# Query projection in units of two batch entries with 256-column matmuls, and value products by half blocks

## The chip, the core and the metric

One NeuronCore of a Trainium2 chip runs the whole kernel. The metric is the device time of one launch in microseconds; three timed runs of the kernel before lie between 2101.3 and 2101.5 us. Everything is computed in float32.

## The reference

One block of a recurrent model on `x` with 8 batch entries of 256 tokens and 512 features: a layer norm, multi-head latent attention with 128 heads, and a feed-forward gate. Cut to what matters here (the FFN gives `g`, and the output is `x + s * g`):

```
c_q  = xn @ Wq_down;  c_kv = xn @ Wkv_down            # latent 64
q_c  = (c_q @ Wq_up).reshape(b, s, 128, 4)            # k_c, v_c from c_kv the same way
q_r  = (xn @ Wq_rope).reshape(b, s, 128, 64)          # 512 x 8192 weights: the largest product
k_r  = xn @ Wk_rope                                    # one 64-wide key for all heads
scores = (q_c . k_c + q_r . k_r) / sqrt(68)
out  = softmax(scores) @ v_c
s    = out.reshape(b, s, 512) @ Wo
```

## The kernel before

There are two stages. The first (`first_phase`) takes the tokens 512 at a time: it normalizes and transposes `x`, makes the latent activations (`down`) and the rope key (`narrow`), and computes the FFN gates into DRAM. Its four passes call `between`, which sets up and starts the second stage: weights, first activations, and in the last pass the first projections.

The second stage is a loop over 64 blocks, `blocks = [(b, sg)]`: one batch entry and 16 of the 128 heads, entry after entry. A block has two halves. One half puts on TensorE (PE), in this order:

- `score` twice (L621): scores of four head groups at a time. Four matmuls with 32 rows each run side by side in the array's four row groups, 256 key columns each. Part 0 is the latent part (`qcm`, `kc`), parts 1 and 2 are the even and odd rope components (`qr`, `act`).
- one `Project` (L162 in `product`): half of the next block's rope queries. The even and odd weight columns, the two halves of the 512 features and the two 128-token halves make a 2 x 2 by 2 x 2 block product, done with seven products instead of eight. Four products go in `first`, three in `second`, each into its own PSUM bank. Each product is four 128x128 weight tiles (`u`, `c`) against 128 token columns. Some of the weights are read with a step of two (`quarter_w`, `w[..., a::2]`); others are sums of weights (`sum_w`, made on GpSimd for the first entry and read back from `sums_d` afterwards). `take` (ScalarE), `join` (GpSimd), the copy in `second` (ScalarE) and `end` (VectorE) put the results together in `qr`.
- at the end of a first half, every second block, `prepare` (L250, L251): the latent queries and keys; `spread` (GpSimd) puts the masked copies in `qcm`.
- at the end of a second half, `weigh` of the block before (L661): value products, with four 32-column weight tiles side by side in the array's column groups, 256 query columns each, summed over eight key groups. Once per entry `values` (L277) makes the values and `place_values` (GpSimd, L292) puts a block's values in `vpad`.

Meanwhile VectorE reduces the maxima (L633), ScalarE makes the exponentials (L639), and VectorE transposes them 32x32 (L649) into `pt`. `normalize` (VectorE) divides, and `finish` (L705) multiplies by `Wo`, multiplies by the gate and adds `x`; it runs in blocks 2 and 3 of the next entry. Each engine follows the written order. All eight PSUM banks are handed out in turn (`bank`): a `score` pair takes eight, a `Project` four, so the banks of the first four scores must have been read by `exponentials` before `first` can begin. Every fp32 matmul of the program is two passes on the PE, each with its own weight load.

All DMAs go through SyncE (SP) in written order: `load_rope` fetches the 1 MB of weights for the half after next, `sum_w` their sums, `load_act` an entry's activations, `load_out` gate and `x` for `finish`.

Of the kernel before, what the change touches and what calls it, by code (L numbers as in the profile page):

```python
# [33 lines left out]
def mla_ffn_gate_kernel(  # L34
# [42 lines left out]
    acts_d = [dram.tile([P, 5, S], F32, name=f"act_d{b}") for b in range(B)]  # L77
    krs_d = [dram.tile([R, TB], F32, name=f"kr_d{n}") for n in range(NTB)]

    sums_d = [dram.tile([P, 4, 2, 2, P], F32, name=f"sums_d{n}") for n in range(16)]  # L80
    gates_d = [dram.tile([P, D], F32, name=f"gate_d{n}") for n in range(NT // P)]

    actp = pool("act", 2)
    wp = pool("wrope", 2)
    qcp = pool("qc", 2)
    qrp = pool("qr", 2)
    vp = pool("v", 2)
    wsp = pool("wsum", 2)
    xsp = pool("xsum", 2)
# [8 lines left out]
    blocks = [(b, sg) for b in range(B) for sg in range(8)]  # L98
    acts, qks, qcms, valls, vpad_of, ropes, qrs = {}, {}, {}, {}, {}, {}, {}

    def load_act(b):
        if b < B:
            acts[b] = actp.tile([P, 7, S], F32, tag="act", name=f"act_{b}")
            nc.sync.dma_start(out=acts[b][:, 0:5, :], in_=acts_d[b])

            kr = krs_d[b // 2].rearrange("(a i) s -> i a s", a=2)[:, :, ds(b % 2 * S, S)]
            for r in range(4):
                nc.sync.dma_start(out=acts[b][32 * r : 32 * r + 32, 5:7, :], in_=kr)

    def load_rope(n, hf):  # L110

        if n < len(blocks):
            t = wp.tile([P, KT, 2, 4 * R], F32, tag="w", name=f"w_{n}_{hf}")
            nc.sync.dma_start(
                out=t.rearrange("p c q m -> p c (q m)"), in_=w_rope[blocks[n][1], hf]
            )
            ropes[n, hf] = t
# [4 lines left out]
    def quarter_w(w, a, k, u):  # L122

        return w[:, 2 * k : 2 * k + 2, u, a::2]

    wsums, xsums = {}, {}

    def sum_w(n, hf):

        if n >= len(blocks):  # L130
            return
        b, sg = blocks[n]
        t = wsp.tile([P, 4, 2, 2, P], F32, tag="ws", name=f"ws_{n}_{hf}")
        if b == 0:
            w = ropes[n, hf]
            q = lambda a, k: w[:, 2 * k : 2 * k + 2, :, a::2]
            nc.gpsimd.tensor_add(t[:, 0], q(1, 0), q(1, 1))
            nc.gpsimd.tensor_sub(t[:, 1], t[:, 0], q(0, 0))
            nc.gpsimd.tensor_sub(t[:, 2], q(0, 0), q(1, 0))
            nc.gpsimd.tensor_sub(t[:, 3], q(0, 1), t[:, 1])  # L140
            nc.sync.dma_start(out=sums_d[2 * sg + hf], in_=t)
        else:
            nc.sync.dma_start(out=t, in_=sums_d[2 * sg + hf])
        wsums[n, hf] = t

    def sum_x(b):

        if b < B:
            t = xsp.tile([P, 4, 2, P], F32, tag="xs", name=f"xs_{b}")
            q = lambda k, tau: acts[b][:, 2 * k : 2 * k + 2, ds(tau * P, P)]  # L150
            nc.gpsimd.tensor_sub(t[:, 0], q(0, 1), q(0, 0))
            nc.gpsimd.tensor_sub(t[:, 1], q(1, 1), t[:, 0])
            nc.gpsimd.tensor_sub(t[:, 2], q(1, 1), q(0, 1))
            nc.gpsimd.tensor_sub(t[:, 3], q(1, 0), t[:, 1])
            xsums[b] = t

    def product(bank_, w, x, first):


        for u in range(2):  # L160
            for c in range(2):
                nc.tensor.matmul(  # L162
                    bank_[:, ds(u * P, P)],
                    w(u)[:, c],
                    x[:, c],
                    start=first and u == 0 and c == 0,
                    stop=c == 1,
                    skip_group_check=True,
                )

    class Project:


        def __init__(self, n, hf):
            self.n, self.hf = n, hf
            self.b = blocks[n][0]
            self.w = ropes[n, hf]
            self.s, self.t = wsums[n, hf], xsums[self.b]
            if hf == 0:

                qrs[n] = qrp.tile([P, 2, 8, 4, 32], F32, tag="qr", name=f"qr_{n}")

            self.banks = []
            self.e = [
                qtp.tile([P, 2 * P], F32, tag=f"e{i}", name=f"e{i}_{n}_{hf}") for i in range(4)
            ]

        def x(self, k, tau):
            return acts[self.b][:, 2 * k : 2 * k + 2, ds(tau * P, P)]

        def a(self, a, k):
            return lambda u: quarter_w(self.w, a, k, u)

        def sums(self, i):
            return lambda u: self.s[:, i, :, u, :]

        def out(self, a, tau):
            q = qrs[self.n][:, a, 4 * tau : 4 * tau + 4, 2 * self.hf : 2 * self.hf + 2, :]
            return q.rearrange("p q u i -> p u q i")

        def split(self, t):
            return t.rearrange("p (u q i) -> p u q i", u=2, i=32)

        def first(self):

            for i, (w, x) in enumerate((
                (self.a(0, 0), self.x(0, 0)),
                (self.sums(1), self.t[:, 1]),
                (self.sums(2), self.t[:, 2]),
                (self.sums(0), self.t[:, 0]),  # L210
# [352 lines left out]
    def between(step):  # L563
# [7 lines left out]
        elif step == 2:  # L571
# [5 lines left out]
            for hf in range(2):  # L577
                sum_w(0, hf)
# [264 lines left out]
```

## Time and profile before

| | |
|---|---|
| median of three runs | 2101.48 us |
| the profiled execution: time, span | 2100.38 us, 2098.6 us |
| first stage | 0 to 231.9 us |
| block loop up to block 63 | 231.9 to 2053.5 us |
| block 63 and what follows | 2053.5 to 2098.6 us |
| PE matmul busy, weight loads busy | 2072.3 us (99%), 1713.9 us (82%) |
| VectorE, ScalarE, GpSimd busy | 1530.7, 1092.8, 713.4 us |
| DMA | 310.99 MB, engines 42% busy in the block loop |
| granted PE clock | 0.998 |

Matmul durations overlap, because a matmul's row runs from its start to its modelled end. The pace of a stream is therefore read from the starts: duration of a merged row less that of one matmul, divided by the number less one. A row's "PE" and "PEld" parts are matmul and weight load.

### The profile page before, as it was taken

How to read it: one execution, taken by the hardware profiler on the slowest of the kernel's cores; microseconds unless marked ns; L12 is line 12 of the kernel's file. 1: busy time of each engine (PE TensorE's matmuls, PEld its weight loads, DVE VectorE, ACT ScalarE, POOL GpSimd, SP SyncE). 2: the span in 40 equal slices, each digit the busy share in tenths (PEclk: the TensorE clock that was granted, in tenths of full speed). 3: DMA queues.
4: the chain of work that ended last, by engine and by line, in shares of the span. 5: the costliest groups of instructions: out<-in, count | busy, mean ns of one | idle time of the engine just before them, and what ended most of it. 6: DMA issues, size and time to landing. Idle time of an engine off the chain costs nothing.

```text
span 2098.6 us, 60067 instructions
## 1 busy us (share of the span) xinstructions
PE 2072.3 (99%) x25024; PEld 1713.9 (82%) x25024; DVE 1530.7 (73%) x2601; ACT 1092.8 (52%) x2989; POOL 713.4 (34%) x989
## 2 busy tenths in 40 slices
PE   7999999999999999999999999999999999999997
PEld 3434888888889888898888988888888888888884
DVE  4332578778687777887777768778787777777875
ACT  2222455555456554564555545555455555554553
POOL 4226566632322233223332332233322333323221
PEclk9999999999999999999999999999999999999999
DMA  4132344343533444334444353444434444334330
GB/s 146 68 133 88 141 162 162 141 189 147 197 134 150 162 164 167 150 134 180 152 162 161 124 205 125 162 161 155 161 139 161 171 160 162 135 149 177 137 132 21
DMA packets 61362, 310.99 MB, mean 148 GB/s; under 512 B 7898, under 2 KB 15706, under 8 KB 28324
## 3 DMA queue, kind: packets, MB, share of 16 engines
q1 hardware_dynamic: 61092, 307.15, 39.3%
q8 instruction: 199, 3.26, 0.6%
q14 instruction: 71, 0.58, 0.1%
HBM read 276.19 MB, written 30.93 MB: 146 GB/s over the span
## 4 chain that ended last, share of the span: by engine, by line
PE 97%; DVE 1%; DMA 1%; POOL 0%; ACT 0%; issue 0%; SPq 0%; POOLq 0%; ACTq 0%; DVEq 0%
PE q L162 40%; PE sc L621 32%; PE av L661 11%; PE po L705 2%; PE px L443 2%; PE py L444 2%; PE pf L486 1%; PE px L429 1%; PE pm L397 1%; PE vps L277 1%; PE qk L250 1%; PE qk L251 1%; PE pp L397 1%; PE pm L458 1%; PE xpt L380 0%; DVE nmx L633 0%
## 5 line engine op out<-in xcount | busy, mean ns | idle before, releaser
L639 ACT ACTIVATE pr<-sc,nmx 128x256 f32<-128x256 f32 x2048 | 819.8, 504 | 415.3 <-DVE nmx L633 414.5
L633 DVE TENSOR_REDUCE nmx<-sc 128x2 f32<-128x512 f32 x1024 | 635.8, 684 | 356.5 <-PE sc L621 329.9
L649 DVE STREAM_TRANSPOSE pt<-pr 128x512 f32<-128x512 f32 x1024 | 635.3, 678 | 0.0
L621 PE MATMUL sc<-act,qr 32*128 32x256 f32 x8192 | 534.6, 374 | 0.0
L621 PEld LDWEIGHTS sc<-act,qr 32*128 32x128 f32 x8192 | 421.1, 185 | 22.1
L221 POOL TENSOR_TENSOR e<-e,e 128x256 f32<-128x256 f32 x128 | 93.2, 729 | 941.3 <-issue 499.9
L162 PE MATMUL q<-xs,ws 128*128 128x128 f32 x3072 | 364.0, 275 | 0.0
L162 PEld LDWEIGHTS q<-xs,ws 128*128 128x128 f32 x3072 | 353.1, 192 | 0.0
L621 PE MATMUL sc<-kc,qcm 32*128 32x256 f32 x4096 | 329.1, 387 | 0.1
L162 PEld LDWEIGHTS q<-act,w 128*128 128x128 f32 x2048 | 261.3, 196 | 44.3 <-ACT pr L639 42.7
L162 PE MATMUL q<-act,w 128*128 128x128 f32 x2048 | 296.2, 288 | 1.1 <-ACT pr L639 1.1
L621 PEld LDWEIGHTS sc<-kc,qcm 32*128 32x128 f32 x4096 | 199.5, 184 | 53.6 <-issue 29.7
L661 PE MATMUL av<-pt,vpad 128*32 128x256 f32 x4096 | 237.4, 382 | 3.8 <-DVE pt L649 2.7
L673 ACT ACTIVATE acc<-av,sides_sb 128x256 f32<-128x256 f32 x128 | 53.8, 471 | 315.2 <-DVE outT L688 161.4
L216 ACT COPY e<-q 128x256 f32<-128x256 f32 x512 | 205.5, 402 | 10.6 <-PE q L162 5.9
L661 PEld LDWEIGHTS av<-pt,vpad 128*32 128x32 f32 x4096 | 128.9, 110 | 89.8 <-issue 3.1
L162 PE MATMUL q<-xs,w 128*128 128x128 f32 x1024 | 141.5, 281 | 0.0
L162 PE MATMUL q<-act,ws 128*128 128x128 f32 x1024 | 135.2, 275 | 0.0
L162 PEld LDWEIGHTS q<-xs,w 128*128 128x128 f32 x1024 | 130.7, 196 | 0.0
L262 POOL TENSOR_TENSOR qcm<-qc,mask_sb 128x1024 f32<-128x1024 f32 x64 | 121.3, 1896 | 20.6 <-ACT qc L253 19.1
L162 PEld LDWEIGHTS q<-act,ws 128*128 128x128 f32 x1024 | 124.4, 192 | 0.0
L292 POOL COPY vpad<-vall 32x128 f32<-32x128 f32 x256 | 78.3, 306 | 95.7 <-PE av L661 51.6
(98 smaller groups left out, 1372.4 us busy)
## 6 DMA issues: line engine op xcount, KB each, us to landing
w<-in_w_rope_dram SPq DMA_DIRECT2D x128, 1024.0 KB
ws<-sums_d SPq DMA_DIRECT2D x112, 1024.0 KB
sums_d<-ws SPq DMA_DIRECT2D x16, 1024.0 KB
act_d<-act SPq DMA_DIRECT2D x8, 640.0 KB
act<-act_d SPq DMA_DIRECT2D x8, 640.0 KB
xt<-in_x_dram SPq DMA_DIRECT2D x16, 256.0 KB
gate_d<-gs SPq DMA_DIRECT2D x16, 256.0 KB
g<-gate_d SPq DMA_DIRECT2D x16, 256.0 KB
```

Of the source, the lines that this page charges most:

```text
L162: nc.tensor.matmul(bank_[:, ds(u * P, P)], w(u)[:, c], x[:, c], start=first and u == 0 and c == 0, stop=c == 1, skip_group_check=True,)
L216: nc.scalar.copy(self.e[i], self.banks[i])
L221: nc.gpsimd.tensor_add(m6, m6, m1)
L262: nc.gpsimd.tensor_mul(qcm, qks[b, sg // 2][0].rearrange("p (q i) -> p q i", i=32).unsqueeze(2).to_broadcast([P, 8, 4, 32]), mask_sb[:, ds ...
L292: nc.gpsimd.tensor_copy(vpad[rows, :, :, 8 * t + 4 * (n % 2) :][..., :4], valls[b][rows, :, sg])
L397: nc.tensor.matmul(ps, weights[:, c, :], xnT[tb][:, c, :], start=(c == 0), stop=(c == KT - 1))
L621: nc.tensor.matmul(sc[r][:, h, :], lhs.rearrange("p t i -> p (t i)"), rhs, start=(part == 0), stop=(part == 2),)
L633: nc.vector.tensor_reduce(nmx[:, r, :], scs[n, f][r], AX.X, ALU.max, negate=True)
L639: nc.scalar.activation(p[:, h, :], scs[n, f][r][:, h, :], AF.Exp, bias=nmxs[n, f][:, r, h : h + 1])
L649: nc.vector.transpose(pts[n, r].rearrange("p k q i -> p q k i")[:, ds(2 * f, 2)], prs.pop((n, f, r)).rearrange("p h (k j) -> p h k j", j=32),)
L661: nc.tensor.matmul(av[32 * r : 32 * r + 32, :S], vpad[:, k, r, :], pt[r][:, k].rearrange("p q i -> p (q i)"), start=(k == 0), stop=(k == 7),)
L673: nc.scalar.activation(a, av[:, :S], AF.Copy, scale=sides_sb[:, side : side + 1])
```

## The change

Blocks are taken in pairs: the two entries of a pair alternate within each `sg`, so `blocks` has entry 2p and 2p+1 of one head group after each other. A unit `j` of `Project` now serves both entries: it covers a quarter of a head group pair's weights and 2 x 256 tokens. The 2 x 2 split over the tokens is now the entry (`e`) and no longer the half of the tokens. A product is two weight tiles against 256 columns instead of four against 128. A block's half still has one unit, but the units run a pair of blocks ahead: `j = 2n + half + 4`, so four units lie in the first stage where two halves lay, and the last two blocks have none.

With it go: weights and sums in pieces of 512 KB (32 sums instead of 16); the activation sums made in the first stage by `sum_x` from `down`, stored as `xs_d`, and read back per pair with `load_xs` into the single buffer of `xsp`; `prepare` two blocks ahead; `values` for two entries in the first stage; the scores' loop with the part outermost; `pt` by half blocks in three buffers; `weigh` in two halves of 128 query columns, moved with `normalize` and `place_values` to the end of the first half; `finish` in second halves of the next pair's blocks 1 to 4, so that both finishes of entry 6 move behind the loop. The core of the diff:

```diff
@@ -74,19 +74,20 @@
     dram = pool("dram", 1, space=bass.MemoryType.DRAM)
-    acts_d = [dram.tile([P, 5, S], F32, name=f"act_d{b}") for b in range(B)]
+    xs_d = [dram.tile([P, 7, 2, S], F32, name=f"xs_d{n}") for n in range(NTB)]
+    cs_d = [dram.tile([P, TB], F32, name=f"cs_d{n}") for n in range(NTB)]
...
-    sums_d = [dram.tile([P, 4, 2, 2, P], F32, name=f"sums_d{n}") for n in range(16)]
+    sums_d = [dram.tile([P, 4, 2, P], F32, name=f"sums_d{n}") for n in range(32)]
-    actp = pool("act", 2)
+    actp = pool("act", 4)
-    qrp = pool("qr", 2)
+    qrp = pool("qr", 4)
-    xsp = pool("xsum", 2)
+    xsp = pool("xsum", 1)
...
+    blocks = [(2 * p + e, sg) for p in range(B // 2) for sg in range(8) for e in range(2)]
+    units = 4 * len(blocks) // 2
...
+    def load_rope(j):
+        if j < units:
+            t = wp.tile([P, KT, 4 * R], F32, tag="w", name=f"w_{j}")
+            sg, u = j // 4 % 8, j % 4
+            nc.sync.dma_start(out=t, in_=w_rope[sg, u // 2][:, :, ds(u % 2 * 4 * R, 4 * R)])
+            ropes[j] = t
+    def sum_w(j):
+        if j < units:
+            t = wsp.tile([P, 4, 2, P], F32, tag="ws", name=f"ws_{j}")
+            if j < 32:
+                q = lambda a, k: ropes[j][:, 2 * k : 2 * k + 2, a::2]
+                nc.gpsimd.tensor_add(t[:, 0], q(1, 0), q(1, 1))
...
+                nc.sync.dma_start(out=sums_d[j], in_=t)
+            else:
+                nc.sync.dma_start(out=t, in_=sums_d[j % 32])
+            wsums[j] = t
+    def sum_x(p, xnT):
+        q = lambda k, e: xnT[:, 2 * k : 2 * k + 2, ds(e * S, S)]
+        t = xsp.tile([P, 7, 2, S], F32, tag="xs", name=f"xt_{p}")
+        nc.gpsimd.tensor_sub(t[:, 3], q(0, 1), q(0, 0))
...
+        for i, of in enumerate((q(0, 0), q(1, 0), q(1, 1))):
+            nc.sync.dma_start(out=xs_d[p][:, i], in_=of)
+        nc.sync.dma_start(out=xs_d[p][:, 3:7], in_=t[:, 3:7])
+    def load_xs(p):
+        if p < B // 2:
+            xsums[p] = xsp.tile([P, 7, 2, S], F32, tag="xs", name=f"xs_{p}")
+            nc.sync.dma_start(out=xsums[p], in_=xs_d[p])
+    def product(bank_, w, x, first):
+        for c in range(2):
+            nc.tensor.matmul(
+                bank_,
+                w[:, c],
+                x[:, c],
+                start=first and c == 0,
+                stop=c == 1,
+                skip_group_check=True,
             )
...
     class Project:
...
+        def __init__(self, j):
+            self.j = j
+            self.n, self.u = 2 * (j // 4), j % 4
+            w, self.s = ropes[j], wsums[j]
+            self.a = lambda a, k: w[:, 2 * k : 2 * k + 2, a::2]
+            self.x = xsums[j // 32]
+            if self.u == 0:
+                for n in (self.n, self.n + 1):
+                    qrs[n] = qrp.tile([P, 2, 8, 4, 32], F32, tag="qr", name=f"qr_{n}")
+            self.e = [qtp.tile([P, S], F32, tag=f"e{i}", name=f"e{i}_{j}") for i in range(4)]
+        def out(self, a, e):
+            return qrs[self.n + e][:, a, :, self.u, :]
...
         def first(self):
...
+            for i, (w, x) in enumerate(
+                ((self.a(0, 0), 0), (self.s[:, 1], 4), (self.s[:, 2], 5), (self.s[:, 0], 3))
+            ):
+                self.banks.append(bank(f"q{i}_{self.j}")[:, 0:S])
+                product(self.banks[i], w, self.x[:, x], True)
@@ -224,10 +210,8 @@
         def second(self):
-            for i, (w, x) in ((0, (self.a(0, 1), self.x(1, 0))),
-                              (2, (self.a(1, 1), self.t[:, 3])),
-                              (3, (self.sums(3), self.x(1, 1)))):
-                product(self.banks[i], w, x, False)
+            for i, w, x in ((0, self.a(0, 1), 1), (2, self.a(1, 1), 6), (3, self.s[:, 3], 2)):
+                product(self.banks[i], w, self.x[:, x], False)
             nc.scalar.copy(self.out(0, 0), self.split(self.banks[0]))
@@ -410,9 +394,10 @@
         def down(tb):
-            nc.scalar.copy(xnT[tb][:, 4, :], over_xn(tb, "pp", wdn_sb))
-            for k in range(2):
-                nc.sync.dma_start(out=acts_d[2 * tb + k], in_=xnT[tb][:, :, ds(k * S, S)])
+            c = f1.tile([P, TB], F32, tag="tmp", name=f"c_{tb}")
+            nc.scalar.copy(c, over_xn(tb, "pp", wdn_sb))
+            nc.sync.dma_start(out=cs_d[tb], in_=c)
+            sum_x(tb, xnT[tb])
         sets, hTs, h4s, mid2ps = {}, {}, {}, {}
...
@@ -565,25 +550,31 @@
             set_up()
         elif step == 1:
             load_act(0)
-            load_rope(0, 0)
-            load_rope(0, 1)
             load_act(1)
+            for j in range(2):
+                load_rope(j)
         elif step == 2:
-            sum_x(0)
             prepare(0, 0)
+            prepare(1, 0)
             spread(0)
             values(0)
+            values(1)
             place_values(0)
-            for hf in range(2):
-                sum_w(0, hf)
-            sum_x(1)
+            sum_w(0)
+            sum_w(1)
+            load_xs(0)
         elif step == 3:
-            Project(0, 0).all()
-            load_rope(1, 0)
+            for j in range(2):
+                Project(j).all()
+                load_rope(j + 2)
+                sum_w(j + 2)
         else:
-            Project(0, 1).all()
-            load_rope(1, 1)
-            sum_w(1, 0)
+            for j in range(2, 4):
+                Project(j).all()
+                load_rope(j + 2)
+                sum_w(j + 2)
+            load_act(2)
+            load_act(3)
...
-    tp = pool("pt", 2)
+    tp = pool("pt", 3)
@@ -609,21 +600,23 @@
-        for h in range(2):
-            q = 2 * f + h
-            for part in range(3):
+        for part in range(3):
+            for h in range(2):
+                q = 2 * f + h
...
-                        lhs, rhs = qr[rows, part - 1, q], a[rows, 4 + part, :]
+                        lhs, rhs = qr[rows, part - 1, q], a[rows, part, :]
                     nc.tensor.matmul(
                         sc[r][:, h, :],
                         lhs.rearrange("p t i -> p (t i)"),
                         rhs,
-                        start=(part == 0),
+                        start=(part == 0 and h == 0),
                         stop=(part == 2),
+                        skip_group_check=True,
                     )
         scs[n, f] = sc
@@ -643,45 +636,49 @@
     def transpose(n, f, r):
-        if f == 0:
-            pts[n, r] = tp.tile([P, 8, 8, 32], F32, tag=f"pt{r}", name=f"pt_{n}_{r}")
+        if f % 2 == 0:
+            pts[n, f // 2, r] = tp.tile([P, 8, 4, 32], F32, tag=f"pt{r}", name=f"pt_{n}_{f}_{r}")
         nc.vector.transpose(
-            pts[n, r].rearrange("p k q i -> p q k i")[:, ds(2 * f, 2)],
+            pts[n, f // 2, r].rearrange("p k q i -> p q k i")[:, ds(2 * (f % 2), 2)],
             prs.pop((n, f, r)).rearrange("p h (k j) -> p h k j", j=32),
         )
     def weigh(n):
-        pt, vpad = [pts.pop((n, r)) for r in range(4)], vpad_of.pop(n)
+        b, sg = blocks[n]
+        vpad = vpad_of.pop(n)
         av = bank(f"av_{n}")
-        for k in range(8):
-            for r in range(4):
-                nc.tensor.matmul(
-                    av[32 * r : 32 * r + 32, :S],
-                    vpad[:, k, r, :],
-                    pt[r][:, k].rearrange("p q i -> p (q i)"),
-                    start=(k == 0),
-                    stop=(k == 7),
-                )
+        for half in range(2):
+            pt = [pts.pop((n, half, r)) for r in range(4)]
+            for k in range(8):
+                for r in range(4):
+                    nc.tensor.matmul(
+                        av[32 * r : 32 * r + 32, ds(half * P, P)],
+                        vpad[:, k, r, :],
+                        pt[r][:, k].rearrange("p q i -> p (q i)"),
+                        start=(k == 0),
+                        stop=(k == 7),
+                        skip_group_check=True,
+                    )
...
@@ -710,20 +707,24 @@
     last = len(blocks) - 1
+    outs = {}
+    for p in range(B // 2 - 1):
+        for i in range(4):
+            outs[16 * p + 17 + i] = 2 * p + i // 2, i % 2
     for n, (b, sg) in enumerate(blocks):
         for half in range(2):
             one, two = 2 * half, 2 * half + 1
-            out_of = b >= 1 and half == 0 and sg in (2, 3)
-            if out_of:
-                load_out(b - 1, sg - 2)
+            j = 2 * n + half + 4
+            if half and n in outs:
+                load_out(*outs[n])
             score(n, one)
             score(n, two)
             maxima(n, one)
             maxima(n, two)
...
-            if n < last:
-                pj = Project(n + 1, half)
+            if j < units:
+                pj = Project(j)
                 pj.first()
@@ -737,37 +738,42 @@
                 transpose(n, one, r)
             for r in range(2):
                 transpose(n, two, r)
-            if n < last:
+            if j < units:
                 pj.end()
             for r in range(2, 4):
                 transpose(n, two, r)
-            if n + 1 + half < len(blocks) and blocks[n + 1 + half][0] == 0:
-                sum_w(n + 1 + half, 1 - half)
-            if n + 2 < len(blocks) and blocks[n + 2][0] > 0:
-                sum_w(n + 2, half)
-            load_rope(n + 2, half)
-            if out_of:
-                finish(b - 1, sg - 2)
+            if j < units and j % 32 == 31:
+                load_xs(j // 32 + 1)
+            if j + 2 < 32:
+                sum_w(j + 1 if j + 1 >= 6 else units)
+            load_rope(j + 2)
+            if j + 2 >= 32:
+                if j + 2 == 32:
+                    sum_w(j + 1)
+                sum_w(j + 2)
             if half == 0:
+                if n + 2 <= last and blocks[n + 2][1] % 2 == 0:
+                    prepare(blocks[n + 2][0], blocks[n + 2][1] // 2)
                 if n < last:
-                    nb, nsg = blocks[n + 1]
-                    if nsg % 2 == 0:
-                        prepare(nb, nsg // 2)
                     spread(n + 1)
-                if sg == 2:
-                    if b >= 1:
-                        load_act(b + 1)
-                        sum_x(b + 1)
-            else:
-                if n % 2 and n >= 2:
+                if n >= 2 and blocks[n - 2][1] % 2:
                     normalize(n - 2)
                 if n >= 1:
                     weigh(n - 1)
-                if sg == 7 and b + 1 < B:
-                    values(b + 1)
-                if n < last:
-                    place_values(n + 1)
+                    place_values(n)
+                if (sg == 7 and b % 2) or (sg == 0 and b and b % 2 == 0):
+                    if b + 1 < B:
+                        values(b + 1)
+                if sg == 2 and b >= 2:
+                    load_act(b + 2)
+            elif n in outs:
+                finish(*outs[n])
+    normalize(last - 1)
+    load_out(B - 2, 0)
+    finish(B - 2, 0)
+    load_out(B - 2, 1)
+    finish(B - 2, 1)
     load_out(B - 1, 0)
     weigh(last)
     normalize(last)
```

## The prediction

> **What bounds the kernel now.** I read the page's busy times, then its chain, then the PE's instructions in order of time, because a busy PE alone doesn't say what in it is slow.
>
> ```profile
> PE 2072.3 (99%) x25024; PEld 1713.9 (82%) x25024; DVE 1530.7 (73%) x2601; ACT 1092.8 (52%) x2989; POOL 713.4 (34%) x989
> PE 97%; DVE 1%; DMA 1%; POOL 0%; ACT 0%; issue 0%; SPq 0%; POOLq 0%; ACTq 0%; DVEq 0%
> PE q L162 40%; PE sc L621 32%; PE av L661 11%; PE po L705 2%; PE px L443 2%; PE py L444 2%; PE pf L486 1%; PE px L429 1%; PE pm L397 1%; PE vps L277 1%; PE qk L250 1%; PE qk L251 1%; PE pp L397 1%; PE pm L458 1%; PE xpt L380 0%; DVE nmx L633 0%
> ```
>
> The chain is the PE nearly throughout, 40% of it the projection. A PE timeline shows one half with a `prepare` before it:
>
> ```profile
> 1022.86 0.59 PE L250 MATMUL qk<-act,wupq_sb 128*128 128x256 f32 x2
> 1023.29 0.59 PE L251 MATMUL qk<-act,wupk_sb 128*128 128x256 f32 x2
> 1023.82 0.71 PE L621 MATMUL sc<-kc,qcm 32*128 32x256 f32 x8
> ...
> 1029.21 1.21 PE L162 MATMUL q<-act,w 128*128 128x128 f32 x8
> 1030.26 2.84 PE L162 MATMUL q<-xs,ws 128*128 128x128 f32 x24
> 1032.94 1.11 PE L162 MATMUL q<-act,w 128*128 128x128 f32 x8
> 1033.88 1.10 PE L162 MATMUL q<-xs,w 128*128 128x128 f32 x8
> 1034.82 1.06 PE L162 MATMUL q<-act,ws 128*128 128x128 f32 x8
> 1035.81 1.50 PE L661 MATMUL av<-pt,vpad 128*32 128x256 f32 x24
> ```
>
> The half costs 5.39 us of scores (1023.82 to 1029.21) and 6.60 of projection (to 1035.81). Nothing waits but at changes of array layout, some 0.2 us each. Passes whose weights lie without a step run at (2.84 - 0.275) / 23 = 112 ns each, weights read with a step of two at (1.11 - 0.281) / 7 = 118 ns. The 256-column passes of `prepare` run at (1023.29 - 1022.86) / 2 = 215 ns; start to start in the trace it is 216. Twice the columns cost less than two passes.
>
> **The change part by part.**
>
> *The unit.* Before: 7 products x 4 tiles x 2 passes = 56 passes, 24 of them with the step (three products of plain weights): 24 x 118 + 32 x 112 = 6.42 us, and 0.2 of switching makes the 6.60 seen. After: 28 passes of 256 columns at 216 ns (the `prepare` row: same 128x128 weights, same columns) = 6.05. That is 0.37 us less, and 128 units give **-47 us**. The step of the weights should cease to matter, since a weight load has 216 ns to hide under.
>
> [...] But the rows have full-height weights at 112 ns for load and matmul together, and 216 for 256 columns, no load on top: the overlap is already there. I take the rows.
>
> *The value products.* 64 passes of 256 columns per block become 128 of 128, so twice the weight loads. The nearest row is `values`, with the same shape:
>
> ```profile
> 918.66 1.93 PE L277 MATMUL vps<-wv_sb,act 128*32 128x128 f32 x64
> 1003.94 3.66 PE L661 MATMUL av<-pt,vpad 128*32 128x256 f32 x64
> ```
>
> Four column tiles form a group, 16 groups a row: `vps` (1.93 - 0.27 - 0.02) / 15 = 109 ns a group, `av` (3.66 - 0.38 - 0.02) / 15 = 217. So 32 x 109 = 3.49 against 16 x 217 = 3.47 us: **+1 us** over 64 blocks, from -6 (the mean pass of `vps` is 26.3 ns) to +6 with a longer switch. [...]
>
> *The load of the activation sums.* `xsp` has one buffer. At a pair's last unit SP waits for its last matmul, then fetches 7 x 2 x 256 x 4 bytes x 128 = 1.84 MB. The next unit's `first` needs it after 5.4 us of scores. Trace: two loads of 1 MB issued at 1035.91 and 1036.28 began moving after 0.8 us and were done 6.7 us after the issue, some 410 GB/s at full rate. So 0.4 + 0.8 + 4.5 + a tail of 1 is 7 us or so: a stall of 1 to 4, three times: **+6** (3 to 12). `load_rope` and `sum_w` are queued behind it on SP; they are needed a half later.
>
> *The end.* Two units move from the end to the first stage and two finishes come to the end. In the last block of before (no projection) DVE sets the pace:
>
> ```profile
> 2056.39 5.08 DVE L633 TENSOR_REDUCE nmx<-sc 128x2 f32<-128x512 f32 x8 [4.67 <-PE sc L621]
> 2061.39 4.85 DVE L649 STREAM_TRANSPOSE pt<-pr 128x512 f32<-128x512 f32 x8
> 2066.16 4.84 DVE L633 TENSOR_REDUCE nmx<-sc 128x2 f32<-128x512 f32 x8
> 2070.92 4.84 DVE L649 STREAM_TRANSPOSE pt<-pr 128x512 f32<-128x512 f32 x8
> ```
>
> 9.7 us a half. Before, block 62 starts at 2025.9 and the end comes 72.7 later. After, from block 62's start: four such halves end at 2.9 + 4 x 9.75 = 41.9; normalize(62) 2.6 to 44.5; the waiting finishes of entry 6 and weigh(63) hold the PE until 52.5; copies, adds, normalize(63) to 57.7; from there to the end as before (2085.68 to 2098.6) 12.9: 70.6. With two units of 6.6 gone and two finishes of 3.4 come, 66.3 would be neutral: **+4** (0 to 9).
>
> *The start.* Four units, a second `prepare` and `values` lie in the first stage; that only moves PE work. New is a knot on POOL, in its written order: the sums for unit 2 stand ahead of the join of unit 1, those for unit 4 ahead of the join of unit 3, each waiting for a load that waits for the unit before. Unit 3's copies wait for join 2, which stands behind the FFN's adds: about 1 us. And SP has two sum stores and ten activation loads (0.43 each) ahead of the last gate stores, so the last gate tiles may free their banks 1 us late: **+2** (0 to 8).
>
> *What I cost at nothing.* POOL: the sums are twice as many at half the size, about 3 us each (four of 0.75, by the 256-column adds of L221); POOL idles 7 us before each join. `sum_x` is four ops of about 1.3 (adds of 512 columns take 1.27) per pass of the first stage, where POOL had 16.9 us free before L469; behind them stand gate stores on SP, and if that cover is gone ScalarE's gate tiles wait, as once before (4.3 us). `place_values` now stands behind `weigh` of the same half, so POOL is held until the PE ends it; the acc adds and the next join are queued behind, the join due 11 us into the next half, POOL free after 4. DMA: weights and sums halve, from an engine share of 42%, not on the chain before. The scores' new order gives `qr` 16 passes (0.86 us) between the unit's end and its first use, more than the 0.5 that `end` takes after the last matmul; the old wait there (8.0 us over 24 times, 0.33 each) equals the layout switch, so no gain.
>
> **Sum**: -47 + 1 + 6 + 4 + 2 = -34 us. Against the profiled 2098.6 (2100.38 with what lies around it) that is 2064.6 and 2066.4; against the median, which is 1.1 higher, 2067.5: I say **2067**.
>
> **The rivals.**
> - *Half blocks become bound by VectorE.* A second half without value products shrinks from 12.0 to 11.6 us, with 10.9 of DVE work in it (5.1 + 4.9 + two `end` adds of 0.42). By the rows DVE waited 1.08 us for scores in such a half (before 2040.81), which leaves 0.7: for it, the slack is thin; against it, it is slack. If those halves can't shrink, 50 x 0.37 = 18 us are lost: 2086.
> - *Slower: the value products are bound per pass, not per column.* At the 54 ns a pass that `av` now has, 8192 passes take 442 us instead of 222: 2287. It turns to slower from 27 + 34 / 8.2 = 31 ns a pass. Against it: `vps`, whose passes differ only in summing nothing.
> - *The change does less than it says*, matmuls split again at 128 columns: excluded by the changed program's instruction list, 14 of 128x256 per unit; each is still two passes.
> - *Loads were partly exposed*: more than -47. Little speaks for it; under 2055.
>
> **How the numbers follow.** The likeliest case 0.73 (own range 2056 to 2078), VectorE-bound halves or late loads up to 2086 0.17, slower 0.05, better than 2055 0.03, and 0.02 that the stalls eat all. Range 2055 to 2086. A measurement can tell about 0.2%, 4 us: faster 0.93, same 0.02, slower 0.05.
>
> **What would show it.** Right: `q` rows of 128x256 at 216 ns start to start, 14 x 2 a unit, 6.2 us from unit to next; `av` groups at 109 ns and 3.5 to 3.7 us a block; a PE wait for the DMA of `xs` three times, 1 to 4 us. Wrong: DVE maxima that no longer wait for scores in second halves; `av` passes near 50 ns; `q` waits for POOL's sums in the first pair.

## The result, and the profile after

| | before | after |
|---|---|---|
| median, us (range) | 2100.91 (2098.98 to 2101.5) | 2093.68 (2090.59 to 2094.74) |
| ratio to before, 95% interval | | 0.9965 (0.9953 to 0.9978) |
| profiled execution: time / span, us | 2100.38 / 2098.6 | 2094.74 / 2093.0 |
| bytes moved by DMA | 310.99 MB | 183.13 MB |

Faster, as forecast, and clear of the noise, but by 7 us (0.35%) and not by 34. 2093.68 lies above the range. The page of the kernel after, the busy line and the first line of its chain (the work that ended last, followed back):

```profile
PE 2046.5 (98%) x25536; PEld 1671.2 (80%) x25536; DVE 1525.3 (73%) x2601; ACT 1085.1 (52%) x2989; POOL 719.2 (34%) x1037
...
PE 94%; DVE 2%; DMA 2%; POOL 1%; issue 0%; SPq 0%; ACT 0%; POOLq 0%; ACTq 0%; DVEq 0%
```

PE fell by 25.8 us of busy time, but it has 94% of the chain where it had 97%: DVE, DMA and POOL now hold it in places. The steady part is what was forecast. PE's timeline after, one half with a unit, and the value products of the next:

```profile
2013.71 1.14 PE L162 MATMUL q<-xs,w 128*128 128x256 f32 x4
2014.69 2.75 PE L162 MATMUL q<-xs,ws 128*128 128x256 f32 x12
2017.28 1.89 PE L162 MATMUL q<-xs,w 128*128 128x256 f32 x8
2019.01 1.03 PE L162 MATMUL q<-xs,ws 128*128 128x256 f32 x4
2019.96 1.15 PE L613 MATMUL sc<-kc,qcm 32*128 32x256 f32 x16
...
2025.36 3.70 PE L657 MATMUL av<-pt,vpad 128*32 128x128 f32 x128
```

A unit takes 6.25 us (2013.71 to 2019.96) instead of 6.60; from the first weight load of a unit to the first of what follows it, the difference is 0.349 us. Its twelve middle passes start (2017.28 - 2014.69) / 12 = 216 ns apart, and passes with the stepped weights (`w`) no longer stand out. The 128 value passes take 3.63 us instead of 3.59.

So the loss lies in the places that occur once or three times. Stretch by stretch, after less before, with work that only moved left out:

| | forecast | measured, us | from |
|---|---|---|---|
| units | -47 | -44.7 | 128 x 0.349 |
| value products | +1 | +3.4 | mean block 3.554 to 3.610, x 61 |
| the start | +2 | +15.0 | first unit of the loop begins at 268.27, before 238.47, 29.8 later; 14.8 of it is moved work: two more units 11.7, a second `prepare` and `values` 3.1 |
| load of activation sums | +6 | +10.4 | scores' stretch before the unit longer by 2.33, 2.24, 3.08; two units of 7.63 instead of 6.25 |
| the end | +4 | +6.7 | block 62's start to the end: 73.0; neutral 66.3 |
| other stretches of scores with a hole or a late end | - | +2.5 | five places, 0.23 to 0.92 |
| rest, with switches of layout | 0 | +1.5 | not traced further |
| sum | -34 | -5.2 | spans: -5.6; 0.4 is not assigned |

**The load of the sums**, first of three: SP's queue of the kernel after, then PE (wait in brackets), then the granted clock and DMA's share by stretches (columns: stretch, length, busy time of PE, PEld, DVE, ACT and POOL with counts, clock, share, GB/s).

```profile
641.39 0.32 SPq L157 DMA_DIRECT2D xs<-xs_d  x1
```

```profile
649.04 1.95 PE L162 MATMUL q<-xs,w 128*128 128x256 f32 x4 [2.29 <-DMA xs<-xs_d]
650.78 3.64 PE L162 MATMUL q<-xs,ws 128*128 128x256 f32 x12
654.26 1.89 PE L162 MATMUL q<-xs,w 128*128 128x256 f32 x8
```

```profile
645.00:649.00 4.00, 1.75 (x36) 1.28 (x28) 3.89 (x7) 3.72 (x10) 0.00 (x0) 1.00 0.97 389
649.20:652.60 3.40, 3.40 (x9) 2.69 (x10) 3.40 (x7) 1.11 (x3) 0.00 (x0) 0.50 0.30 117
652.60:656.00 3.40, 3.40 (x18) 3.04 (x17) 0.34 (x1) 2.35 (x8) 0.00 (x0) 1.00 0.00 0
```

The wait is the forecast one. New is what follows it: 3.4 us at a clock of 0.50 (called half clock from here on), in which PE does half as many matmuls as in the next 3.4 us (9 against 18). A wait of 2.3 us costs 3.7: the wait and 1.4 that the unit behind it takes longer.

**The start** has three losses. The first lies in the first pass of the feed-forward (pass 0). POOL after, then DVE after, whose last line is the same instruction a pass later, then DVE before in pass 0:

```profile
36.74 1.28 POOL L146 TENSOR_TENSOR xt<-act 128x512 f32<-128x512 f32 x1
38.10 1.27 POOL L147 TENSOR_TENSOR xt<-act,xt 128x512 f32<-128x512 f32 x1
...
41.79 1.44 POOL L454 TENSOR_TENSOR h<-hT 128x512 f32<-128x512 f32 x1
```

```profile
40.65 5.67 DVE L353 TENSOR_SCALAR xt<-xt,mv,rstd 128x512 f32<-128x512 f32 x4
46.24 2.69 DVE L432 TENSOR_TENSOR hT<-gate,py 128x512 f32<-128x512 f32 x4
...
94.62 1.91 DVE L353 TENSOR_SCALAR xt<-xt,mv,rstd 128x512 f32<-128x512 f32 x4
```

```profile
37.48 3.77 DVE L369 TENSOR_SCALAR xt<-xt,mv,rstd 128x512 f32<-128x512 f32 x4
```

The four `tensor_scalar`s of the norm take 5.67 us while POOL subtracts and adds, 3.77 in before's pass 0, where POOL has only its adds, and 1.91 with POOL still. The small DVE instructions ahead of them (128x4) are held in the same way: up to 1.18 us each, where they take 0.16 with POOL still. The `hT` products behind them start 5.1 us later than before (46.24 against 41.17). Of this, 1.4 us is there before POOL subtracts (the norm begins at 33.09 against 31.74): the clock of this execution came up at 17.7 us, before's at 13.6 (the eight `pm` passes that start at 14.07 take 5.47 us, before's eight from 14.52 on 3.67). The other 3.7 is DVE beside POOL. ACT's gates and PE wait, and a half clock follows (0.50 from 48.4 to 51.8), which makes it 6.7 by the first `prepare` (190.4 against 183.7).

The second and third, ACT after, then SP's queue:

```profile
241.87 0.37 ACT L202 COPY e<-q 128x256 f32<-128x256 f32 x1 [6.83 <-POOL e L207]
...
262.49 1.18 ACT L475 ACTIVATE gs<-pf 128x512 f32<-128x512 f32 x2 [9.60 <-DMA gate_d<-gs]
```

```profile
253.83 0.32 SPq L136 DMA_DIRECT2D sums_d<-ws  x1
254.20 0.43 SPq L109 DMA_DIRECT2D act<-cs_d  x1
254.68 2.21 SPq L113 DMA_DIRECT2D act<-kr_d  x4
256.93 0.42 SPq L109 DMA_DIRECT2D act<-cs_d  x1
257.40 1.84 SPq L113 DMA_DIRECT2D act<-kr_d  x4
259.34 4.67 SPq L476 DMA_DIRECT2D gate_d<-gs  x4
```

Unit 3's copies wait for unit 2's join (`e`, L207), which stands on POOL behind the feed-forward's adds: units 2 and 3 take 16.7 us instead of the 12.4 of two units (+4.3). And the gate stores stand on SP until 259.34, behind a store of sums and ten loads of activations; ACT waits 9.6 us with the last two gates, and their banks are those of the first scores, whose stretch takes 10.94 us instead of 6.57 (+4.4). A half clock follows each of these two waits of PE of 2.49 and 2.51 us (0.51 from 242.92 to 246.33 and from 263.40 to 266.81). The three losses add to 15.4; the table's 15.0 takes off the moved work, which is known to some tenths only.

**The end**, PE after:

```profile
2063.94 7.11 PE L702 MATMUL po<-wo_sb,outT 128*128 128x512 f32 x10 [7.79 <-DVE outT L685]
2070.98 3.70 PE L657 MATMUL av<-pt,vpad 128*32 128x128 f32 x128
2074.61 2.84 PE L702 MATMUL po<-wo_sb,outT 128*128 128x512 f32 x6
```

PE follows the written order: it waits 7.79 us for `normalize(62)`, the last value products (2070.98) stand behind that, and the ten passes that follow the wait run at half clock (0.50 from 2058.9 to 2069.1): 7.11 us, where before's last ten take 4.56.

### The profile page after: what moved, and what is told of

Read it like the earlier page. It is cut to its first block, busy times and chain, and to the rows that moved or that the text cites. A ratio compares the mean times of both kernels' runs of the same rounds, so it can differ in the third digit from the quotient of the medians.

```text
span 2093.0 us, 61071 instructions
## 1 busy us (share of the span) xinstructions
PE 2046.5 (98%) x25536; PEld 1671.2 (80%) x25536; DVE 1525.3 (73%) x2601; ACT 1085.1 (52%) x2989; POOL 719.2 (34%) x1037
## 2 busy tenths in 40 slices
DMA packets 110262, 183.13 MB, mean 87 GB/s; under 512 B 8154, under 2 KB 80474, under 8 KB 108964
## 4 chain that ended last, share of the span: by engine, by line
PE 94%; DVE 2%; DMA 2%; POOL 1%; issue 0%; SPq 0%; ACT 0%; POOLq 0%; ACTq 0%; DVEq 0%
PE q L162 38%; PE sc L613 31%; PE av L657 11%; PE po L702 2%; PE px L428 2%; PE py L429 2%; PE pf L471 1%; PE px L414 1%; DMA xs<-xs_d 1%; DVE pt L642 1%; DVE nmx L626 1%; PE pm L381 1%; PE vps L261 1%; PE qk L234 1%; PE qk L235 1%; PE pp L381 1%
## 5 line engine op out<-in xcount | busy, mean ns | idle before, releaser
L613 PE MATMUL sc<-act,qr 32*128 32x256 f32 x8192 | 493.8, 375 | 0.2 <-issue 0.2
L162 PE MATMUL q<-xs,ws 128*128 128x256 f32 x2048 | 486.7, 381 | 0.0
L207 POOL TENSOR_TENSOR e<-e,e 128x256 f32<-128x256 f32 x128 | 93.2, 728 | 1089.1 <-ACT e L202 568.9
L162 PEld LDWEIGHTS q<-xs,ws 128*128 128x128 f32 x2048 | 391.4, 191 | 52.5 <-issue 0.2
L162 PE MATMUL q<-xs,w 128*128 128x256 f32 x1536 | 389.7, 390 | 10.3 <-DMA xs<-xs_d 7.5
L162 PEld LDWEIGHTS q<-xs,w 128*128 128x128 f32 x1536 | 292.3, 197 | 80.1 <-ACT pr L632 44.3
L613 PE MATMUL sc<-kc,qcm 32*128 32x256 f32 x4096 | 287.5, 388 | 2.6 <-ACT gs L475 2.5
L657 PE MATMUL av<-pt,vpad 128*32 128x128 f32 x8192 | 236.8, 273 | 1.2 <-ACT pr L632 1.2
L657 PEld LDWEIGHTS av<-pt,vpad 128*32 128x32 f32 x8192 | 219.7, 110 | 22.9 <-POOL e L208 8.0
L209 POOL TENSOR_TENSOR qr<-e,e 128x256 f32<-128x256 f32 x128 | 93.8, 732 | 10.0
L208 POOL TENSOR_TENSOR e<-e,e 128x256 f32<-128x256 f32 x128 | 93.5, 730 | 10.0
L219 DVE TENSOR_TENSOR qr<-e,q 128x256 f32<-128x256 f32 x128 | 54.0, 422 | 44.5 <-POOL e L207 34.0
```

What stands on the lines that cost most here:

```text
L162: nc.tensor.matmul(bank_, w[:, c], x[:, c], start=first and c == 0, stop=c == 1, skip_group_check=True,)
L207: nc.gpsimd.tensor_add(m6, m6, m1)
L208: nc.gpsimd.tensor_add(m7, m7, m6)
L209: nc.gpsimd.tensor_add(self.out(1, 1), self.split(m7), self.split(m5))
L613: nc.tensor.matmul(sc[r][:, h, :], lhs.rearrange("p t i -> p (t i)"), rhs, start=(part == 0 and h == 0), stop=(part == 2), skip_group_chec ...
L657: nc.tensor.matmul(av[32 * r : 32 * r + 32, ds(half * P, P)], vpad[:, k, r, :], pt[r][:, k].rearrange("p q i -> p (q i)"), start=(k == 0), ...
```

## The experiments

Each is timed beside the kernel before, on the same chip; ratios are to it, with 95% intervals. Differences "than after" are of medians from different sessions, and by these intervals good to 3 or 4 us.

**e1: the activation sums in two tiles.** `xs` becomes `xa` (parts 0, 3, 4, 5, which `first` reads) and `xb` (1, 2, 6, which `second` reads).

```
 pj.first()
+if j % 32 == 31: load_xa(j // 32 + 1)
 ...
-    load_xs(j // 32 + 1)
+    load_xb(j // 32 + 1)
```

> The changed kernel, with the activation sums of a pair in two tiles: the four that the first products read (1.05 MB) are fetched as soon as the last unit's first products are through, the other three (0.79 MB) when its second products are. Theory A (the gain was given back at seams, this one worth three waits of 2.3, 2.2 and 3.1 us for the load and twice 1.4 us of half-speed PE after it): no PE wait for these loads is left, no half clock there, and the time falls by 8 to 10 us, to about 2083. Theory B (the wait only uncovers another, ScalarE or VectorE a little behind): the waits for the load go, but the half in question stays over 6 us from scores to projection, and the time falls by less than 4 us.

2082.74 us, ratio 0.9917 (0.9903 to 0.993): 10.9 less than after. PE at the same place:

```profile
644.28 1.91 PE L620 MATMUL sc<-act,qr 32*128 32x256 f32 x32
646.12 1.14 PE L169 MATMUL q<-xa,w 128*128 128x256 f32 x4
```

No wait, and no half clock from 267 us to 2048 (mean granted clock 0.994, after 0.992). The term is 10.4 by the trace and 10.9 by the medians, not 6.

**e2: the last value products first.**

```
-normalize(last - 1)
 load_out(B - 2, 0)
-finish(B - 2, 0)
 load_out(B - 2, 1)
+weigh(last)
+normalize(last - 1)
+finish(B - 2, 0)
 ...
```

and two buffers each for `g` and `xr`.

> The changed kernel with another end: the last value products stand ahead of the two finishes of entry 6, normalizations follow, and gate and x have two buffers each. Theory A (the end lost 7 us, because the PE waits in order on the finishes, runs them at half clock, and the four loads of gate and x go one after the other, 7 us each): last value products at once when VectorE has done its last transpose, and 6 to 9 us less, about 2086. Theory B (the end is bound by VectorE's chain of 4 x 9.7 us and what hangs on it): under 3 us.

2088.0 us, ratio 0.9936 (0.9924 to 0.9949): 5.7 less than after, a little under what was expected. The order and the second buffers were changed together, so their shares are not known. PE still waits there, but once and for less:

```profile
2061.13 5.15 PE L657 MATMUL av<-pt,vpad 128*32 128x128 f32 x64 [4.24 <-DVE pt L642]
```

**e3: the changed kernel with each product split again into 2 x 128 columns.**

```
+for u in range(2):
     for c in range(2):
-        nc.tensor.matmul(bank_, w[:, c], x[:, c], ...)
+        nc.tensor.matmul(bank_[:, ds(u * P, P)], w[:, c], x[:, c, ds(u * P, P)], ...)
```

> The changed kernel with each 256-column product split in two of 128 columns, everything else in its new place: 56 passes a unit again. Theory A (the wide products did bring 0.35 us a unit, and the loss is elsewhere): a unit goes from 6.25 back to about 6.6 us, and the time rises by 40 to 47 us, to about 2137, over the kernel before by the 37 that the seams cost. Theory B (the wide products bring little in the loop, since something else takes the place, such as VectorE in the halves without value products): the time rises by under 20 us.

2139.73 us, ratio 1.0183 (1.0169 to 1.0197): 46 more than after. The unit is 6.60 us again. The wide columns did bring what was forecast (47); the rest of the change took most of it back.

**e4: the kernel before with value products in halves of 128 columns**, at their old place.

```
-for k in range(8):
-    for r in range(4):
-        nc.tensor.matmul(av[32 * r : 32 * r + 32, :S], ...)
+for hf in range(2):
+    for k in range(8):
+        for r in range(4):
+            nc.tensor.matmul(av[32 * r : 32 * r + 32, ds(hf * P, P)], ...)
```

> The kernel before with only the value products narrowed to 128 columns, 128 passes a block instead of 64, at their old place. Theory A (paid by columns, as the rows of the values' own projection said): groups of four at 105 to 109 ns, 3.55 to 3.7 us a block instead of 3.59, the time within 6 us of the kernel before. Theory B (part of the loss is here, by a price per pass): 4 us a block or more, 25 us and over on the whole.

2118.02 us, ratio 1.0076 (1.0062 to 1.009): 17 more than before, which neither theory had. The value products themselves take 3.63 us a block, 0.04 more. But in 14 of the 123 halves of the loop the scores behind them have a hole of over 0.5 us; the sum of all scores' stretches is 677.8 us, before 663.3. One such place, PE:

```profile
1157.16 3.70 PE L662 MATMUL av<-pt,vpad 128*32 128x128 f32 x128
1160.68 1.93 PE L277 MATMUL vps<-wv_sb,act 128*32 128x128 f32 x64
1162.54 0.71 PE L621 MATMUL sc<-kc,qcm 32*128 32x256 f32 x8
1163.07 0.59 PE L621 MATMUL sc<-act,qr 32*128 32x256 f32 x3
1164.66 0.92 PE L621 MATMUL sc<-act,qr 32*128 32x256 f32 x11 [1.00 <-issue]
```

The hole falls in the middle of one group of scores, and PE waits for no engine and no data ("issue"). The DMA queues of e4 in the 6 us from 1158 on (packets, MB, share of the 16 engines):

```profile
q1 hardware_dynamic: 278, 2.06, 90.3%
q8 instruction: 1, 0.02, 1.0%
```

The DMA engines are full of weights, and one piece of PE's program came through. e4 has 8192 more PE instructions than before, and its instruction queue moves 231 pieces of 16 KB where before's moves 199: 256 instructions a piece. The 192 narrow passes above with as many weight loads are 384 instructions in 5.4 us. That made a theory, tried in e11.

**e11: the kernel of e4 without its later loads of weights.**

```
+if n >= 8: ropes[n, hf] = ropes[7, hf]     # load_rope
+if n >= 8: wsums[n, hf] = wsums[7, hf]     # sum_w
```

> The kernel of e4 (before, with value products by halves of 128 columns) with the loads of weights and of weight sums left out from block 8 on: blocks 8 to 63 use the tiles of block 7, so what they compute is not the reference. Theory F (the holes of 0.5 to 1.7 us in the scores behind e4's value products come from PE's instructions arriving late: 256 more of them per block than before, fetched in 16 KB pieces that queue behind the 2 MB of weights just asked for): without these loads the holes go, the scores' segments sum to within 3 us of before's 663 us (e4: 678), and the time is 2101 to 2107. Rival G (the holes come from the value products themselves, whose narrow passes leave less time for the scores' loads): the scores still sum to 673 us or more, and the time stays within 4 us of e4's 2118.

2103.09 us, ratio 1.0011 (1.0004 to 1.0017). The scores sum to 663.3 us, before's figure, and their longest segment in the loop is 5.393. The holes need the loads: rival G fell, and theory F holds as far as that. The two traces also bear on the fetch. In all 14 halves of e4 the hole ends 1.3 to 1.6 us after a piece of the instruction queue has landed, and that piece begins to move when PE is 128 to 220 instructions further in its program than at the same piece in e11 (median over all pieces: 48). The pieces themselves take no longer (median 0.98 us in e4's loop, 1.12 in e11's). So the fetch comes late and the holes end with it; why it begins late beside the loads, no run shows.

**e5: the sums of pass 0 later.** `sum_x(0)`, subtractions and stores, behind the first group of adds.

```
-sum_x(tb, xnT[tb])                         # in down
+if tb > 0: sum_x(tb, xnT[tb])
 ...
         low_out(tb, u // 2 - 1)
+    if u == 2 and tb == 0: sum_x(tb, xnT[tb])
```

> The changed kernel with one thing moved: the four POOL subtractions and four stores that make the first pass's activation sums (sum_x of pass 0) are issued behind the first group of adds of pass 0 (low_out at u 2) instead of ahead of it. Theory A (the start lost 5 us of its 15 because these 5 us of POOL work stand ahead of the first L454 adds, which hold hT, which holds DVE and ACT's gates): the wait of 7.67 us of ACT's gates on DVE's hT shrinks to 2 us or less, the half clock at 48 us goes, the second prepare starts 4 to 6 us sooner, and the time is 4 to 6 us below the changed kernel's 2093.7. Rival B (POOL has no room for the sums anywhere in pass 0): the same wait appears at the next group of adds (u 4), the time stays within 1.5 us of the changed kernel. Rival C (the pass began late for the clock alone): nothing moves before 60 us.

2102.8 us, ratio 1.0008 (1.0 to 1.0016): 9 more than after, which none of the three theories had. The adds did come first, at 35.53. But DVE's four `tensor_scalar`s (L353) took 5.66 us all the same, since the subtractions now ran beside them. And the three stores of the activations had moved with the sums, behind four loads of `x` that wait for buffers. SP's queue, then ACT:

```profile
29.74 30.93 SPq L300 DMA_DIRECT2D xt<-in_x_dram  x4
60.72 1.54 SPq L151 DMA_DIRECT2D xs_d<-act  x3
```

```profile
65.79 1.07 ACT L367 COPY act<-xpt 128x512 f32<-128x512 f32 x2 [6.62 <-DMA xs_d<-act]
```

The next pass can't write its activations until these are stored. The order on POOL was thus not the cause of the first 5 us: theory A of e5 fell.

**e9: the subtractions beside products from PSUM.** The three activation stores stay in `down`; subtractions and their store go to u 4, where DVE multiplies gates by `py` out of PSUM.

```
+store_x(tb, xnT[tb])                       # in down
+if tb > 0: sum_x(tb, xnT[tb])
 ...
+    if u == 4 and tb == 0: sum_x(tb, xnT[tb])
```

> The changed kernel with the four POOL subtractions of pass 0's activation sums behind the second group of adds (u 4), where DVE only multiplies gates by a PSUM operand, and with the three stores of the activations themselves left where they were on SP's queue (e5 had moved them behind the four loads of x, at 60.7 us, which held the activation buffer and ACT's copy for 6.6 us). Theory A (the 5 us were not POOL's order against its own adds, but DVE's norm of the next pass: four tensor_scalars of 128x512 from SBUF to SBUF take 1.91 us with POOL still, 5.67 us with POOL's subtractions beside them, one after the other): the four take 3.8 us as before, the gates' wait falls from 7.67 us to about 4, PE's wait of 2.3 us and the half clock at 48 us go, and the second prepare starts 5 to 7 us sooner than in the changed kernel, at 184 to 185.5 us; the time is 4 to 7 us below 2093.7. Rival B (any place in pass 0 costs as much): no gain over 1.5 us.

2087.77 us, ratio 0.9936 (0.9924 to 0.9948): 5.9 less than after; the `prepare`s of the first stage start at 184.3 instead of 190.4, 1.0 of it there before POOL's adds in pass 0 (the norm's last statistics start at 34.54, after's at 35.50). DVE, then POOL:

```profile
39.92 1.92 DVE L354 TENSOR_SCALAR xt<-xt,mv,rstd 128x512 f32<-128x512 f32 x4
...
47.97 0.68 DVE L435 TENSOR_TENSOR hT<-gate,py 88x512 f32<-88x512 f32 x1 [1.00 <-PE py L432]
```

```profile
47.15 1.27 POOL L149 TENSOR_TENSOR xt<-act 128x512 f32<-128x512 f32 x1
```

The norm's four take 1.92 us, less than the 3.8 expected, since POOL's first adds now end at 39.86, just ahead of them. The product with a PSUM operand takes 0.68 with POOL's subtractions beside it (47.97), as it does in after with POOL still (0.68 at 52.41). The norm's `tensor_scalar`s, from SBUF to SBUF, take 0.48 us apiece with POOL still (1.91 / 4) and 1.42 beside POOL's subtractions (5.67 / 4); one POOL subtraction takes 1.27. Why the one is slowed and the other not, no run shows.

**e6: the feed-forward's last adds ahead of units 0 to 3.**

```
-between(3)
 low_out(tb, 2)
+between(3)
 between(4)
```

> The changed kernel with the last group of products and POOL adds of the feed-forward's last pass (low_out, n = 2) issued ahead of projection units 0 and 1 instead of behind them. Theory A (units 2 and 3 took 16.7 us instead of 12.4 because join 2 stood on POOL behind these adds): ACT's wait of 6.83 us on POOL's e in unit 3 and PE's of 2.49 us go, and with them the half clock at 243 us; the time falls by 3 to 5 us from 2093.7. Rival B (the products then wait for the gates of u 5 that units 0 and 1 used to cover): PE waits 3 us or more for hT ahead of unit 0, and the time stays within 1.5 us or rises.

2094.6 us, ratio 0.9972 (0.996 to 0.9984): no gain. What was aimed at went: PE no longer waits in unit 3. The first scores then waited more. ACT:

```profile
238.10 0.37 ACT L202 COPY e<-q 128x256 f32<-128x256 f32 x1 [3.45 <-POOL e L207]
...
261.13 1.27 ACT L475 ACTIVATE gs<-pf 128x512 f32<-128x512 f32 x2 [13.21 <-DMA gate_d<-gs]
```

The gate stores go out no sooner, so the earlier gates wait 13.2 us for them instead of 9.6, and PE 6.13 instead of 2.51. Rival B was right about the time and wrong about the place.

**e7: the gate stores ahead of the sum of unit 5 and of the activation loads.** `sum_w(5)`, `load_act(2)` and `load_act(3)` go from `between(4)` to behind `gate_out`.

> The changed kernel with the sum of weights of unit 5 (POOL work and its store) and the loads of two batch entries' activations issued behind the gate stores instead of ahead of them. Theory A (the first gate stores stood on SP's queue behind a store that waits for POOL and ten loads, which held gs, ACT and through it the first scores): ACT's wait of 9.60 us on the gate's store falls below 3 us, PE's 2.51 us ahead of the first scores goes, with the half clock at 263.5 us; 3 to 5 us less than 2093.7. Rival B (the gates' stores end late because of their own transfer, two buffers for four stores): the wait stays above 5 us and the time within 1.5 us.

2088.84 us, ratio 0.9938 (0.9926 to 0.9951): 4.9 less than after. ACT's gates no longer wait for the gate stores; the fourth now waits for PE:

```profile
256.91 0.60 ACT L475 ACTIVATE gs<-pf 128x512 f32<-128x512 f32 x1 [1.98 <-PE pf L471]
```

**e8 and e10: all five together**, e8 with the place of e5 for the sums, e10 with that of e9.

> The changed kernel with all five together: activation sums in two tiles fetched half a unit apart, value products of the last block ahead of the normalizing and finishing of the one before it with two buffers for gate and input rows, the sums of pass 0 later, the last adds of the feed-forward ahead of units 0 to 3, and the gate stores ahead of sum of unit 5 and activation loads. Theory A (the losses are separate stretches in which PE stood or ran at half clock, and add): 10.9 and 5.7 as measured for the first two, and 4 to 6, 3 to 5 and 3 to 5 for the others make 27 to 33 us less than the changed kernel, 2061 to 2067, near the 2067 that was predicted with a start and an end at nearly no cost. Rival B (with one hole closed another takes its place): the sum falls short by 8 us or more, 2075 or above.

> The kernel with all five edits, its sums of pass 0 placed as in e9 instead of as in e5. Theory A (losses add): 2074.6 less the 7.9 us that e5's place cost against the changed kernel, less the 4 to 7 us that e9's place is to bring, makes 2060 to 2063. Rival B (another hole takes its place): 2066 or above.

e8: 2074.63 us, ratio 0.9872 (0.9858 to 0.9885), 7.6 short of theory A's 2067 and at rival B's bound; e5's loss of 9 is in it. e10: 2065.14 us (2063.4 to 2067.8), ratio 0.983 (0.9818 to 0.9843): 28.5 less than after, the fastest of all. The single gains of e1, e2, e9 and e7 add to 27.4 (10.9 + 5.7 + 5.9 + 4.9), so the losses add as far as these differences can tell; whether e6's edit brings anything beside e7's was not run. e10 came out between its two bounds: e8 less e5's and e9's difference would be 2060. In the profiled executions e10 takes 2.5 us more than e8 between the first `prepare` and the end, 1.6 of it in longer stretches of scores (6.82 against 5.95 us in the first). Behind its first matmul, PE's two longest waits in e10 are (total, times, longest):

```profile
PE av L673 <- DVE pt L658: 4.2, 1, 4.2
PE q L172 <- ACT pr L648: 1.4, 1, 1.4
```

No wait for `xs` or `gs` is left, and 0.2 us for `e`; once the clock is up, at 19 us, it is at a half only in the end, from 2036.7 (mean granted clock 0.998).

## Why the prediction was right in sign and wrong in size

The step that failed is the start: two waits priced at 1 us each and `sum_x` at nothing. Beside it, no term of the sum had the half clock: by the excesses measured behind the waits it cost some 11 us in all (an estimate: 1.4 to 1.9 at five places and 2.7 in the end), over a third of what was missed.

- *The unit*: right. -44.7 by the trace against -47, and 46 by e3. Reading 216 ns off the `prepare` rows held: the unit's middle passes start 216 ns apart too, with their weight loads (191 ns each) beside them and not on top.
- *The value products*: their own time lies in the forecast's 3.5 to 3.7 (3.63 us). Missed: twice as many of their instructions have to be fetched (128 passes a block instead of 64; in e4 the instruction queue moves 231 pieces instead of 199). That goes with 14.5 us of holes in e4; here, with half the weights to load, the longer stretches of scores come to 2.5 us, which is the most it can have cost in the loop.
- *The load of the sums*: right mechanism, size 10.4 instead of 6. The waits, 7.65 together, lie within the 1 to 4 each; 2.8 is the half clock behind two of them.
- *The end*: 6.7 instead of 4. `normalize(62)` was put at 44.5 us from block 62's start and came at 44.0 (2063.94). PE was to be held until 52.5 and was until 54.7 (2074.61), since the ten passes after the wait ran at half clock.
- *The start*: 15.0 instead of 2 and beyond its bound of 8. Unit 3's wait and the gate stores were both named, in the right order, at 1 us each; they cost 4.3 and 4.4, because a wait on ACT of 6.8 and 9.6 us reaches PE as 2.5 and is followed by a half clock each time. And `sum_x`, costed at nothing since "POOL had 16.9 us free before L469", cost 5.3 in pass 0 (the 6.7 less the clock's 1.4): I looked at POOL's idle time in the steady passes, while pass 0 has `set_up` ahead, and at POOL's order, not at which DVE instructions run beside POOL's.
- *The rivals*: VectorE did not become the bound; it still waits for scores (0.93 and 0.94 us in such halves). No mean pass was near 31 ns (3.63 us / 128 = 28).
- e10 runs in 2065, near the forecast of 2067, but not by the forecast's own terms: these granted 12 us to the loads, the start and the end, and e10 takes away the loads' waits altogether. The nearness is in part luck.

## What to carry to other kernels

Where PE is the bound, price a short wait of PE with the half clock that can follow it (here 1.4 to 1.9 us more behind waits of 2.3 to 3.0), not by its length alone. Work for an "idle" POOL is not free when DVE works between SBUF tiles at that time (here 5.67 us instead of 1.91), and what is added to SP's queue delays the stores behind it, whose buffers other engines wait for (here ACT, 9.60 us). When a large gain vanishes, list stretches of PE in order of time, before and after: here 32 of the 39 us lost lay in the first 270 us, at three loads and at the end.

## What the hardware showed beyond that

- PE waits of 2.3 to 3.0 us were followed by 3.41 us of half clock at 48, 243, 263, 649 and 1567 us of after; one of 2.2 us at 1106 was not. In other runs waits of 2.87 us (e9), 2.93 (e7) and 3.04 (e2), all at the third load, were not followed by one, and one of 2.22 us (e7) was, so the length alone doesn't decide. In the trace of after each of these five half clocks lasts 3.413 us, and the starts of all seven, the two of the end among them, lie 194.56, 20.48, 385.71, 918.19, 491.52 and 27.31 us apart: 57, 6, 113, 269, 144 and 8 times 3.413, each to within 0.03 of a step. Why they lie so, no run shows.
- PE's program can come late where data fill the DMA engines: in e4, with passes 27 ns apart and 2 MB of weights under way (90.3% of the DMA engines), scores' stretches grew by 14.5 us in all. In e11, with the same passes and without those loads, they did not (663.3 us, as before).
- Traffic fell by 41%, from 310.99 to 183.13 MB, and no stretch of PE is seen to have become faster by it. Stretches of scores over 0.5 us too long, other than at the three loads: 2 in after's loop, 14 in e4's, which has the loads of before and also more PE instructions than after.
